# A Mamba-like macaron block on one core: x times B for four states at once, the clip and all products on GpSimd, one projection, new places in the order

## The chip, the cores and the metric

The kernel runs on one core of one Trainium2 chip. The core has four compute engines that work side by side and each take their instructions in a fixed order: TensorE (PE in the profile; its weight loads are listed as PEld), VectorE (DVE), ScalarE (ACT) and GpSimd (POOL). SyncE (SP) issues the transfers. An instruction waits on semaphores for its operands and buffers, and what stands behind it in its engine's queue waits with it. The metric is the device time of one execution in microseconds (us). Before the change it is 3603.74 us, the median of three executions (3602.82 to 3605.33).

## The reference

The input x is 32 sequences ("batches") of 512 positions and 256 channels, fp32. A block has three parts, each with a residual:

```python
x = x + 0.5 * ffn(layernorm(x))
x = x + ssm(layernorm(x))
x = x + 0.5 * ffn(layernorm(x))
```

The FFN has 704 hidden channels, and its inputs and weights go through a 4-bit quantization in blocks of 16 (scale = largest absolute value / 6, value = nearest of eight grid points, times scale):

```python
h = silu(q(x) @ q(w_gate).T) * (q(x) @ q(w_up).T)
out = q(h) @ q(w_down).T
```

The state-space part has N = 16 states per channel. A is -1 to -16, A and dt are fp32:

```python
Bm, Cm = split(x @ W_in + b_in)                  # 16 columns each
dt = softplus((x @ W_dt1 + b_dt1) @ W_dt2 + b_dt2)   # through 64 columns
dt = clip(dt, 1e-7, 1e6)
A_bar = exp(A * dt)                              # per channel and state
B_barX = expm1(A * dt) / (A * dt) * dt * Bm * x
h[t] = A_bar[t] * h[t-1] + B_barX[t]             # along the 512 positions
out = sum over states (h * Cm) + D * x
```

## The kernel before

**Tiling.** One batch is handled as four row tiles of 128 positions (`NJ`), or, in the state-space part, as two column halves of 128 channels (`NC`) by 512 positions. Everything is fp32 except the quantizer's curve, which is bf16. The weights of the FFN are loaded, quantized and transposed once, at the start (three blocks of gate and up rows, two blocks of down rows).

**The FFN** (`ffn`): a layernorm, `quantize` of the 128x1024 activations, two transposes, and then for each row tile: gate projections in two halves of 352 columns (line 676) with silu on ScalarE, up projections, the product of both, `quantize` of the 128x704 result, transposes (710), the down projection (722) and a copy out (729). The product is made by GpSimd (699) after two ScalarE copies of up out of PSUM (696); for tile 0 of the first FFN alone (`BY_DVE`) VectorE makes it straight from PSUM (692) without these copies.

**`quantize`**: VectorE takes the largest value of each block (544), the scale (546), its reciprocal (548) and the quotient (550, into PSUM); ScalarE squares and bends it (554, 556); TensorE adds and subtracts a large constant, which rounds to the grid (563); ScalarE copies out (569); GpSimd multiplies by the scale (570). The quotient lives in one PSUM buffer, "q", of which there is one, so two quantizations follow each other.

**The state-space part** (`ssm`): a layernorm, transposes, one projection for B and C (741 with `w_in_sb`, bias 745) and one to the 64 columns of dt (741 with `w_dt1_sb`, bias 752), from there dt (757), softplus on ScalarE within PSUM (761) and the clip on VectorE out of PSUM into SBUF (764). B and C are written to DRAM and come back, spread over all 128 partitions, two states at a time (780, 782). For each pair of states of a column half: exp and tanh by ScalarE (789, 792), x times B by GpSimd (796), and for each state three VectorE instructions: e (803), e times x B (806) and the scan along the positions (809). GpSimd multiplies the pair by C (812), and TensorE adds it, turned, to the sum over the states in PSUM (818). expm1 is had from exp and tanh: exp(2z) - 1 = (exp(2z) + 1) tanh(z).

x times B is one GpSimd instruction for two states and 512 positions (1024 columns), written with the state as the innermost index, so that one x element is used twice in a row:

```python
op("POOL", "x b", lambda c=c, bx=bx, bn=bn: g.tensor_tensor(
    bx().rearrange("p n l -> p l n"),
    xT()[:, c, :].unsqueeze(2).to_broadcast([P, L, NG]),
    bn().rearrange("p n l -> p l n"), ALU.mult),
```

**The order.** Nothing is issued at once. `op` records each instruction with its reads and writes, and `Plan.run` puts all of them, of all batches, in one list: of those whose inputs have been issued and whose buffers are free it always takes the one with the smallest place. The place is the entry of its name in the table `WHEN` plus `PERIOD` times its batch. So every batch has the same places, shifted, and work of several batches is interleaved: in the steady stage the FFN 0 of one batch, the state-space part of the one before it and FFN 1 of an older one run together. A place is no time; only the order follows from it, and the numbers of buffers (three PSUM buffers "pt" for all projections, transposes and small things, one "q", two or three of the others) bound how far an engine runs ahead. The list is fixed before the kernel runs. The first batch has a fill stage ahead of it, where the weights are quantized, and the last a drain.

The functions that the change touches follow, with the line numbers that the profile uses.

Of the kernel before, what the change touches and what calls it, by code (L numbers as in the profile page):

```python
# [9 lines left out]
F32 = mybir.dt.float32  # L10
# [6 lines left out]
P = 128  # L17
# [14 lines left out]
        "weights load": (7249, 7248, 7249, 7249, 6726, 6726, 6642, 6642, 6642, 6841, 6841, 6841,  # L32
        6841),
        "weights x top": (7249, 7065, 7353),
        "weights x scale": (7250, 7248, 7385),
        "weights x rinv": (7250, 7248, 7391),
        "weights x quotient": (7250, 7248, 7391),
        "weights x square": (7250, 7249, 7392),
        "weights x curve": (7250, 7249, 7392),
        "weights x grid": (7250, 7249, 7557),  # L40
        "weights x rounded": (7250, 7249, 7557),
        "weights x value": (7250, 7249, 7558),
        "weights turn": (7251, 7251, 7249, 7249, 7558, 7558),
        "weights turned": (7251, 7251, 7250, 7251, 7558, 7558),
        "weights load down": (7065, 6579),
        "weights h top": (7558, 6642),
        "weights h scale": (7571, 6642),
        "weights h rinv": (7571, 6642),
        "weights h quotient": (7571, 6643),
        "weights h square": (7590, 6643),  # L50
        "weights h curve": (7590, 6643),
        "weights h grid": (7590, 6643),
        "weights h rounded": (7590, 6643),
        "weights h value": (7795, 7065),
        "weights turn down": (7795, 7795, 7699, 7661),
        "weights turned down": (7897, 7814, 8179, 7699),
        "weights zero rows": (8077, 8345),
        "in load": (0,),
        "ffn 0 stats": (1267, 1773, 601, 2361),
        "ffn 0 mean": (1913, 2355, 1536, 3584),  # L60
        "ffn 0 var + eps": (4038,),
        "ffn 0 rstd": (4045,),
        "ffn 0 - mean": (3609,),
        "ffn 0 shift": (4249,),
        "ffn 0 normal": (4499, 5056, 6579, 4467),
        "ffn 0 x top": (6643,),
        "ffn 0 x scale": (6726,),
        "ffn 0 x rinv": (6822,),
        "ffn 0 x quotient": (6835,),
        "ffn 0 x square": (6841,),  # L70
        "ffn 0 x curve": (6873,),
        "ffn 0 x grid": (6880,),
        "ffn 0 x rounded": (6950,),
        "ffn 0 x value": (6969,),
        "ffn 0 xqT turn": (7065, 7129),
        "ffn 0 xqT turned": (7136, 7168),
        "ffn 0 tile 0 gate": (7353, 7251),
        "ffn 0 tile 0 silu": (7437, 7321),
        "ffn 0 tile 0 up": (7577, 7558),
        "ffn 0 tile 0 up silu": (7584, 7571),  # L80
        "ffn 0 tile 0 h top": (7590,),
        "ffn 0 tile 0 h scale": (7609,),
        "ffn 0 tile 0 h rinv": (7661,),
        "ffn 0 tile 0 h quotient": (7705,),
        "ffn 0 tile 0 h square": (7737,),
        "ffn 0 tile 0 h curve": (7808,),
        "ffn 0 tile 0 h grid": (7814,),
        "ffn 0 tile 0 h rounded": (7897,),
        "ffn 0 tile 0 h value": (8045,),
        "ffn 0 tile 0 turn h": (8301, 8192),  # L90
        "ffn 0 tile 0 turned h": (8352, 8339),
        "ffn 0 tile 0 down": (8397,),
        "ffn 0 tile 0 sum": (8461,),
        "ffn 0 tile 1 gate": (7385, 7392),
# [187 lines left out]
        "ffn 1 tile 3 sum": (18157,),  # L282
        "out store": (19712,),
}


class Buf:

# [598 lines left out]
```

## Time and profile before

| What | Value |
|---|---|
| Median of three executions | 3603.74 us |
| The profiled execution | 3604.13 us, span 3602.2 us |
| Granted TensorE clock over the span | 0.984 of full |
| First softplus table load / last | 123.7 us / 3408.7 us |
| Out stores, first and last issue | 395.7 us / 3598.4 us |
| Busy: PE / DVE / ACT / POOL | 3348.0 / 3409.9 / 3385.7 / 3332.3 us |
| Instructions: PE / DVE / ACT / POOL | 16604 / 5280 / 5813 / 1963 |

The page adds up the busy time of each engine over the whole span, fill and drain included; the windows view gives the same for a chosen stretch. A row of the costliest groups reads: line, engine, operation, tiles written and read, shapes and count, then the total busy time in us and the mean duration of one in ns, and last the engine's idle time just before these instructions with what ended it. A row of the waits reads: engine, tile and line that waited, what ended the wait, us in total, times, longest. Instructions of one engine overlap a little at their ends, so a group's busy time can be under its count times the mean.

### The profile page before, as it was taken

The numbers are of one execution on the slowest core, as the hardware profiler recorded it, in microseconds if no ns is written. First come the engines' busy times: TensorE is split into PE (matmuls) and PEld (weight loads), VectorE is DVE, ScalarE is ACT, GpSimd is POOL, SyncE is SP. The second block draws the span as 40 slices with busy tenths as digits, with TensorE's granted clock in tenths as the row PEclk, the third lists the DMA queues.
The fourth block names the chain that finished last, engine by engine and source line by source line (L and its number), as shares of the span: only waits on it lengthen the run. The fifth ranks groups of instructions, "written<-read, shape, count | busy, mean of one in ns | idle before, by whom it ended". The sixth has DMA issues, their size and how long they took to land. (4 is left out here: it accounts for less than half of the span.)

```text
span 3602.2 us, 51333 instructions
## 1 busy us (share of the span) xinstructions
PE 3348.0 (93%) x16604; PEld 2443.6 (68%) x16826; DVE 3409.9 (95%) x5280; ACT 3385.7 (94%) x5813; POOL 3332.3 (93%) x1963
## 2 busy tenths in 40 slices
PE   5779999999999999999999999999999999999966
PEld 3457777667767767777766776776777776777654
DVE  3699999999999999999999999999999999999992
ACT  4689999999999999999999999999999999999973
POOL 2589999999999999999999999999999999999992
PEclk9899999999999999999999999999999999999988
DMA  1354545444545545454544454444555454445440
GB/s 45 112 173 166 173 164 176 165 169 165 176 171 170 165 158 175 170 173 164 177 165 169 165 176 170 170 165 159 176 171 173 163 177 165 168 161 169 171 170 12
DMA packets 186652, 578.36 MB, mean 161 GB/s; under 512 B 19664, under 2 KB 54032, under 8 KB 186384
## 3 DMA queue, kind: packets, MB, share of 16 engines
q1 hardware_dynamic: 184816, 574.89, 46.7%
q8 instruction: 133, 2.18, 0.2%
q14 instruction: 135, 1.11, 0.1%
q10 hardware_dynamic: 1568, 0.18, 0.0%
HBM read 556.12 MB, written 18.87 MB: 160 GB/s over the span
## 5 line engine op out<-in xcount | busy, mean ns | idle before, releaser
L676 PE MATMUL pt<-w_guT,xqT 128*128 128x352 f32 x4096 | 1317.4, 466 | 26.1 <-DVE dt L764 16.3
L812 POOL TENSOR_TENSOR hs<-hs,bc 128x1024 f32<-128x1024 f32 x512 | 1214.0, 2371 | 9.3 <-DVE hs L809 2.6
L809 DVE TENSOR_TENSOR_SCAN hs<-ab,eb 128x512 f32<-128x512 f32 x1024 | 1202.4, 1197 | 4.5
L796 POOL TENSOR_TENSOR bx<-xT,bc 128x1024 f32<-128x1024 f32 x512 | 1171.2, 2294 | 30.3 <-DVE eb L806 15.9
L676 PEld LDWEIGHTS pt<-w_guT,xqT 128*128 128x128 f32 x4096 | 753.3, 192 | 409.7 <-DVE dt L764 24.0
L792 ACT ACTIVATE eb<-dt,a_half 128x512 f32<-128x512 f32 x1024 | 708.1, 700 | 36.1 <-DVE hs L809 29.5
L806 DVE SCALAR_TENSOR_TENSOR eb<-eb,a_inv,bx 128x512 f32<-128x512 f32 x1024 | 734.9, 743 | 2.7
L722 PE MATMUL pt<-w_dT,hqT 128*128 128x256 f32 x3072 | 717.0, 383 | 14.8 <-ACT hqT L715 14.8
L789 ACT ACTIVATE ab<-dt,a_sb 128x512 f32<-128x512 f32 x1024 | 700.8, 727 | 1.5
L803 DVE SCALAR_TENSOR_TENSOR eb<-ab,eb 128x512 f32<-128x512 f32 x1024 | 684.5, 682 | 11.4 <-ACT eb L792 7.6
L722 PEld LDWEIGHTS pt<-w_dT,hqT 128*128 128x128 f32 x3072 | 580.1, 192 | 140.4 <-ACT hqT L715 32.9
L818 PE MATMUL py<-ident,hs 128*128 128x128 f32 x4096 | 536.1, 276 | 26.1 <-POOL hs L812 25.8
L818 PEld LDWEIGHTS py<-ident,hs 128*128 128x128 f32 x4096 | 469.4, 142 | 102.0 <-POOL hs L812 38.3
L570 POOL TENSOR_TENSOR h_q<-h_q,h_sc 128x704 f32<-128x704 f32 x258 | 360.3, 1397 | 53.2 <-ACT h_q L569 52.6
L699 POOL TENSOR_TENSOR h<-h,sl 128x704 f32<-128x704 f32 x224 | 379.0, 1692 | 27.4 <-ACT h L696 22.4
L544 DVE TENSOR_REDUCE q<-h 128x44 f32<-128x704 f32 x258 | 227.0, 880 | 68.6 <-POOL h L699 43.8
L710 PE MATMUL pt<-ident,h_q 128*128 128x128 f32 x1536 | 237.0, 278 | 41.2 <-ACT h L696 24.1
L563 PE MATMUL q<-h_m,eye 128*128 128x192 bf16 (+1 forms) x873 | 191.6, 305 | 70.9 <-ACT h_m L556 62.0
L710 PEld LDWEIGHTS pt<-ident,h_q 128*128 128x128 f32 x1536 | 180.5, 141 | 110.3 <-ACT h L696 51.8
L563 PEld LDWEIGHTS <-eye 128*128 128x128 bf16 x1300 | 125.2, 99 | 183.9 <-issue 106.8
L715 ACT COPY hqT<-pt 128x256 f32<-128x256 f32 (+1 forms) x512 | 233.9, 487 | 6.1 <-PE pt L710 5.7
L686 ACT ACTIVATE sl<-pt 128x352 f32<-128x352 f32 x512 | 222.5, 463 | 16.6 <-PE pt L676 13.8
(78 smaller groups left out, 4134.6 us busy)
## 6 DMA issues: line engine op xcount, KB each, us to landing
bc<-rows SPq DMA_DIRECT2D x1024, 512.0 KB, 4.1
x<-in_L_attn_x_dram SPq DMA_DIRECT2D x32, 512.0 KB, 5.2
out_dram<-x SPq DMA_DIRECT2D x32, 512.0 KB, 7.3
rows<-bc SPq DMA_DIRECT2D x32, 64.0 KB, 3.4
xn<-in_L_ffn_w_up_dram SPq DMA_DIRECT2D x6, 128.0 KB, 2.2
h<-in_L_ffn_w_down_dram SPq DMA_DIRECT2D x2, 352.0 KB, 3.4
xn<-in_L_ffn_w_gate_dram SPq DMA_DIRECT2D x5, 128.0 KB, 2.2
w_dt_sb<-in_L_attn_W_dt_dram ACTq DMA_DIRECT2D x2, 64.0 KB, 5.5
```

The costliest lines, as they stand in the source:

```text
L676: pe.matmul(to()[:, :HALF], lhsT=xqT()[:, c, j * P : (j + 1) * P], rhs=w_guT()[:, c, o : o + HALF], start=(c == 0), stop=(c == NC - 1),)
L699: op("POOL", "product", lambda sl=sl, h=h: g.tensor_tensor(h(), h(), sl(), ALU.mult), [h, sl], [h])
L710: pe.transpose(pt()[:, i * P : (i + 1) * P], hq()[:, kcol[k] : kcol[k] + P], ident)
L722: pe.matmul(po()[:, :DM], lhsT=hqT()[:, k, :], rhs=w_dT()[:, k, :], start=(k == 0), stop=False,)
L789: op("ACT", "exp", lambda c=c, i=i, k=k, ab=ab: s.activation(ab()[:, i, :], dt()[:, c, :], AF.Exp, scale=a_sb[:, c, k : k + 1]), [(dt, c)] ...
L792: op("ACT", "tanh", lambda c=c, i=i, k=k, eb=eb: s.activation(eb[i](), dt()[:, c, :], AF.Tanh, scale=a_half[:, c, k : k + 1]), [(dt, c)], ...
L796: op("POOL", "x b", lambda c=c, bx=bx, bn=bn: g.tensor_tensor(bx().rearrange("p n l -> p l n"), xT()[:, c, :].unsqueeze(2).to_broadcast([P ...
L803: op("DVE", "e", lambda i=i, ab=ab, eb=eb: v.scalar_tensor_tensor(eb[i](), ab()[:, i, :], 1.0, eb[i](), ALU.add, ALU.mult), [(ab, i), eb[i ...
L806: op("DVE", "e x b", lambda c=c, i=i, k=n + i, eb=eb, bx=bx: v.scalar_tensor_tensor(eb[i](), eb[i](), a_inv[:, c, k : k + 1], bx()[:, i, : ...
L809: op("DVE", "scan", lambda i=i, h=h, ab=ab, eb=eb: v.tensor_tensor_scan(h()[:, i, :], ab()[:, i, :], eb[i](), 0.0, ALU.mult, ALU.add), [(a ...
L812: op("POOL", "h c", lambda h=h, cn=cn: g.tensor_tensor(flat(h()), flat(h()), flat(cn()), ALU.mult), [h, cn], [h])
L818: pe.matmul(py()[:, j, :], lhsT=h()[:, i, j * P : (j + 1) * P], rhs=ident, is_transpose=True, start=False, stop=False, skip_group_check=True,)
```

## The change

- **x times B** (`XG = 4`): B is loaded for four states at a time, one transfer in the place of two. GpSimd multiplies in two instructions per group of four states, each over all four states and half of the positions, with the four states innermost. Both have 1024 columns, so the number of instructions and columns per batch stays as it was (16 and 16384). C still comes two states at a time. There are two buffers of B and two of the result, each for four states.
- **The clip of dt**: softplus writes SBUF instead of PSUM, and GpSimd clips there, in place, with one instruction per column half, in place of VectorE.
- **The products**: `PRODUCT_BY_DVE` is empty. GpSimd makes the product of tile 0 of the first FFN too, and ScalarE makes the two copies of up ahead of it. (`VALUE_BY_DVE` is empty as well, so the scale product stays on GpSimd.)
- **One projection**: the weights of dt and of B and C stand side by side in one tile of 96 columns; one pair of matmuls, one PSUM buffer and one bias instruction make both.
- **The places**: all entries of `WHEN` are new, and the plan has tables of their own for the first two and the last two batches (`FIRST`, `SECOND`, `LAST_BUT_ONE`, `LAST`). `PERIOD` stays 3379.

The numbers in the tables are left out below.

```diff
-WHEN = { ... }
+WHEN = { ... }
+FIRST = { **WHEN, ... }
+SECOND = { **WHEN, ... }
+LAST_BUT_ONE = { **WHEN, ... }
+LAST = { **WHEN, ... }
+
+PRODUCT_BY_DVE = set()
+VALUE_BY_DVE = set()
+CLIP_BY = "POOL"
...
-    def __init__(self):
-        self.ops, self.slots = [], {}
+    def __init__(self, tables):
+        self.ops, self.slots, self.tables = [], {}, tables
...
-        o.at = (WHEN[o.name][k] + self.batch * PERIOD, len(self.ops))
+        table = self.tables.get(self.batch, WHEN)
+        o.at = (table[o.name][k] + self.batch * PERIOD, len(self.ops))
...
     NG = 2
+    XG = 4
     PT = 3
...
-    w_in_sb = const.tile([P, NC, 2 * N], F32, name="w_in_sb")
-    w_dt1_sb = const.tile([P, NC, R], F32, name="w_dt1_sb")
+    w_p_sb = const.tile([P, NC, R + 2 * N], F32, name="w_p_sb")
     w_dt2_sb = const.tile([R, DM], F32, name="w_dt2_sb")
-    b_in_sb = const.tile([2 * N, 1], F32, name="b_in_sb")
-    b_dt1_sb = const.tile([R, 1], F32, name="b_dt1_sb")
+    b_p_sb = const.tile([R + 2 * N, 1], F32, name="b_p_sb")
...
-    BY_DVE = {(0, 0)}
...
-    plan = Plan()
+    plan = Plan({0: FIRST, 1: SECOND, NB - 2: LAST_BUT_ONE, NB - 1: LAST})
...
-                if (which, j) in BY_DVE:
+                if (which, j) in PRODUCT_BY_DVE:
...
-        def project(to, w):
+        def project():
             for c in range(NC):
-                pe.matmul(to, lhsT=w[:, c, :], rhs=xT()[:, c, :], start=(c == 0), stop=(c == NC - 1))
-
-        op("PE", "bc", lambda: project(pbc()[: 2 * N, :], w_in_sb), [xT], [pbc])
-        bc = new(sp, [2 * N, L], F32, "bc", 1)
-        op("ACT", "bc bias", lambda: s.activation(
-            bc(), pbc()[: 2 * N, :], AF.Identity, bias=b_in_sb), [pbc], [bc])
+                pe.matmul(pbc()[: R + 2 * N, :], lhsT=w_p_sb[:, c, :], rhs=xT()[:, c, :],
+                          start=(c == 0), stop=(c == NC - 1))
+
+        op("PE", "project", project, [xT], [pbc])
+        bc = new(sp, [R + 2 * N, L], F32, "bc", 1)
+        op("ACT", "project bias", lambda: s.activation(
+            bc(), pbc()[: R + 2 * N, :], AF.Identity, bias=b_p_sb), [pbc], [bc])
         rows = new(dr, [2 * N, L], F32, "rows", 2)
-        op("SP", "rows", lambda: nc.sync.dma_start(rows(), bc()), [bc], [rows])
-        p1 = new(ps, [P, L], F32, "pt", PT)
-        op("PE", "dt1", lambda: project(p1()[:R, :], w_dt1_sb), [xT], [p1])
-        r1 = new(sp, [R, L], F32, "r1", 1)
-        op("ACT", "dt1 bias", lambda: s.activation(
-            r1(), p1()[:R, :], AF.Identity, bias=b_dt1_sb), [p1], [r1])
+        op("SP", "rows", lambda: nc.sync.dma_start(rows(), bc()[R:, :]), [bc], [rows])
         dt = new(sp, [P, NC, L], F32, "dt", 2)
         p2 = [new(ps, [P, L], F32, "pt", PT) for _ in range(NC)]
         for c in range(NC):
             op("PE", "dt2", lambda c=c: pe.matmul(
-                p2[c](), lhsT=w_dt2_sb[:, c * P : (c + 1) * P], rhs=r1(), start=True, stop=True),
-               [r1], [p2[c]])
+                p2[c](), lhsT=w_dt2_sb[:, c * P : (c + 1) * P], rhs=bc()[:R, :],
+                start=True, stop=True), [bc], [p2[c]])
         for c in range(NC):
-            op("ACT", "softplus", lambda c=c: s.activation(
-                p2[c](), p2[c](), AF.Softplus, bias=b_dt2_sb[:, c : c + 1]),
-               p2[c:], [p2[c]])
-            op("DVE", "dt", lambda c=c: v.tensor_scalar(
-                dt()[:, c, :], p2[c](), 1e-7, 1e6, ALU.max, ALU.min), [p2[c]], [(dt, c)])
+            if CLIP_BY == "POOL":
+                op("ACT", "softplus", lambda c=c: s.activation(
+                    dt()[:, c, :], p2[c](), AF.Softplus, bias=b_dt2_sb[:, c : c + 1]),
+                   p2[c:], [(dt, c)])
+                op("POOL", "dt", lambda c=c: g.tensor_scalar(
+                    dt()[:, c, :], dt()[:, c, :], 1e6, 1e-7, ALU.min, ALU.max),
+                   [(dt, c)], [(dt, c)])
...
             for n in range(0, N, NG):
-                bn, cn = (new(st, [P, NG, L], F32, f"bc{i}", 2) for i in range(2))
-                op("SP", "load b", lambda n=n, bn=bn: nc.sync.dma_start(
-                    bn(), rows()[n : n + NG, :].partition_broadcast(P)), [rows], [bn])
+                if n % XG == 0:
+                    bn, bx = (new(st, [P, XG, L], F32, tag, 2) for tag in ("bn", "bx"))
+                    op("SP", "load b", lambda n=n, bn=bn: nc.sync.dma_start(
+                        bn(), rows()[n : n + XG, :].partition_broadcast(P)), [rows], [bn])
+                    for o in range(0, L, L * NG // XG):
+                        t = slice(o, o + L * NG // XG)
+                        op("POOL", "x b", lambda c=c, bx=bx, bn=bn, t=t: g.tensor_tensor(
+                            bx()[:, :, t].rearrange("p n l -> p l n"),
+                            xT()[:, c, t].unsqueeze(2).to_broadcast([P, L * NG // XG, XG]),
+                            bn()[:, :, t].rearrange("p n l -> p l n"), ALU.mult),
+                           [(xT, c), bn], [(bx, o)])
+                cn = new(st, [P, NG, L], F32, "cn", 2)
                 op("SP", "load c", lambda n=n, cn=cn: nc.sync.dma_start(
                     cn(), rows()[N + n : N + n + NG, :].partition_broadcast(P)), [rows], [cn])
...
-                bx = new(st, [P, NG, L], F32, "bx", 2)
-                op("POOL", "x b", lambda c=c, bx=bx, bn=bn: g.tensor_tensor(
-                    bx().rearrange("p n l -> p l n"),
-                    xT()[:, c, :].unsqueeze(2).to_broadcast([P, L, NG]),
-                    bn().rearrange("p n l -> p l n"), ALU.mult),
-                   [(xT, c), bn], [bx])
...
                     op("DVE", "e x b", lambda c=c, i=i, k=n + i, eb=eb, bx=bx: v.scalar_tensor_tensor(
-                        eb[i](), eb[i](), a_inv[:, c, k : k + 1], bx()[:, i, :],
+                        eb[i](), eb[i](), a_inv[:, c, k : k + 1], bx()[:, k % XG, :],
                         ALU.mult, ALU.mult), [eb[i], bx], [eb[i]])
```

## The prediction

> **What bounds the kernel now.** I read the page's first two parts, then a window over ten batches, then the waits in that window, then the costliest groups with shapes kept apart, and last the two ends.
>
> The page, part 1 and the first rows of part 2 (busy us, share, instructions; tenths in 40 slices of 90 us):
> ```profile
> PE 3348.0 (93%) x16604; PEld 2443.6 (68%) x16826; DVE 3409.9 (95%) x5280; ACT 3385.7 (94%) x5813; POOL 3332.3 (93%) x1963
> ...
> DVE  3699999999999999999999999999999999999992
> ACT  4689999999999999999999999999999999999973
> POOL 2589999999999999999999999999999999999992
> ```
> Four engines look alike because the ends are averaged in. Softplus loads its table once per batch. The row of line 761 for a middle window (1000 to 2200 us), and the windows view over the ten batches that it marks:
> ```profile
> L761 ACT ACT_TABLE_LOAD  x11: 1283/1283/1283, 1070.7 to 2134.9; - x11
> ```
> ```profile
> 1070.70:2134.80 1064.10, 1027.29 (x5172) 753.63 (x5240) 1058.12 (x1641) 1049.80 (x1811) 1038.24 (x611) 1.00 0.50 169
> ```
> Eleven loads from 1070.7 to 2134.9 us are ten batches of 106.41 us. After the window's length stand PE, PEld, DVE, ACT, POOL, then the clock. Per batch: DVE 105.8, ACT 105.0 to 105.1, POOL 103.8, PE 102.7. The waits in the same window: VectorE has none, and ScalarE's are
> ```profile
> ACT x L729 <- PE pt L726: 2.9, 10, 0.3
> ACT xn_s L522 <- POOL shift L519: 2.2, 10, 0.2
> ACT eb L792 <- DVE hs L809: 2.0, 10, 0.2
> ```
> So VectorE sets the pace: 105.8 us of work and 0.6 us between instructions make 106.41 us. ScalarE follows 0.9 us behind: 105.1 us of work and 0.4 us of gaps under 60 ns make 105.5 us, and the rest of its time is waiting that VectorE's pace causes. GpSimd has 2.6 us to spare, TensorE 3.6.
>
> **The change, part by part**, in us per batch of the steady stage. The groups that price it:
> ```profile
> L812 POOL TENSOR_TENSOR hs<-hs,bc 128x1024 f32<-128x1024 f32 x512 | 1214.0, 2371 | 9.3 <-DVE hs L809 2.6 <-DMA bc<-rows 1.5 <-PE pt L676 1.2
> L796 POOL TENSOR_TENSOR bx<-xT,bc 128x1024 f32<-128x1024 f32 x512 | 1171.2, 2294 | 30.3 <-DVE eb L806 15.9 <-DMA bc<-rows 14.2
> L699 POOL TENSOR_TENSOR h<-h,sl 128x704 f32<-128x704 f32 x224 | 379.0, 1692 | 27.4 <-ACT h L696 22.4 <-issue 2.7 <-DVE h_sc L546 1.6
> L696 ACT COPY h<-pt 128x352 f32<-128x352 f32 x448 | 191.2, 450 | 7.9 <-PE pt L676 7.6
> L570 POOL TENSOR_TENSOR x_q<-x_q,x_sc 128x1024 f32<-128x1024 f32 x67 | 129.7, 1936 | 60.5 <-ACT x_q L569 60.5
> L741 PE MATMUL pt<-xT,w_in_sb 128*32 128x512 f32 x128 | 60.9, 598 | 0.0
> L764 DVE TENSOR_SCALAR dt<-pt 128x512 f32<-128x512 f32 x64 | 40.4, 671 | 14.9 <-ACT pt L761 14.9
> L692 DVE TENSOR_TENSOR h<-pt,sl 128x352 f32<-128x352 f32 x64 | 32.8, 512 | 13.3 <-PE pt L676 10.2
> L752 ACT ACTIVATE r<-pt,b_dt_sb 64x512 f32<-64x512 f32 x32 | 22.2, 693 | 2.2 <-PE pt L741 2.2
> L745 ACT ACTIVATE bc<-pt,b_in_sb 32x512 f32<-32x512 f32 x32 | 21.2, 664 | 1.2 <-PE pt L741 1.2
> ```
> *VectorE* loses the clip (40.4/32 = 1.26) and the two products of tile 0 of the first FFN (32.8/32 = 1.02): 106.41 - 2.28 = 104.1. It stops being the bound.
>
> *ScalarE* gains two up copies in their place (2 x 191.2/448 = +0.85) and loses one of the two bias instructions (21.2/32 = -0.66; the merged one has 96 rows, and the rows of 32 and 64 take nearly the same, 664 and 693 ns). Softplus, writing SBUF instead of PSUM, I leave at its 662 ns. The list of the changed kernel has nine table loads per steady batch, as before, and three more in the whole run (one in the fill, two in the drain, 1.28 us each, beside idle ScalarE time there). So its floor is 105.5 + 0.2 = 105.7: the next bound is only 0.7 us below the old one.
>
> *TensorE* loses one projection, 60.9/32 = 1.9: 102.8 + 0.4 - 1.9, about 101.3. It sets nothing. Softplus into SBUF also frees a PSUM slot one step earlier; TensorE waited 5.2 us for the clip's in ten batches, time that it has to spare.
>
> *GpSimd* gains the product of tile 0 (+1.69) and two clips, and its x times B changes shape. The number of x-times-B instructions (16) and their elements (1024) stay; the innermost run is 4 states, with x repeated 4 times, instead of 2. No row shows either price.
> - Clip, 128x512, one input: from below, the only one-input operation here (the identity's affine select, 292 ns for 128 columns, less the 203 ns of a 4-column tensor_tensor, is 0.70 ns a column): 0.56 us. From above, at the two-stream rate of the 1024-column h times c ((2371 - 203)/1024 = 2.12 ns): 1.29 us. I take 0.75, nearest to the one-input row (0.87 with the 98 ns memset as its fixed part).
> - x times B: from above 2371 ns, two full streams without any repeat; from below 1936 ns, the scale product, whose second operand is repeated 16 times. Repeats of 2 give 2294. With the fixed 203 ns off, that is 2.04 ns a column at 2 and 1.69 at 16; halfway in doublings, one of three steps, gives 1.92 at 4: 2.17 us. I take it; 16 x (2.17 - 2.294) = -2.0.
>
> Sum: 103.8 + 1.7 + 1.5 - 2.0 = 105.0; with the ends of both prices 100.9 to 109.3. At the taken values GpSimd lies 0.7 us under ScalarE, with no spare time for much waiting.
>
> The Trainium skill, "GPSIMD Engine Reference", section "Performance pitfalls for Q7 kernels", says that reads with a step over 8 bytes cost about 2.9 instead of 1.9 cycles an element. x times B steps by 2048 bytes in both kernels, and its 2294 ns lie under the 2371 ns of the contiguous h times c, so this trace doesn't show the penalty. By the rule (1.2 GHz on the same page) an estimate is 2.7 us each, 113 us of GpSimd work per batch, and a kernel of about 3790 us.
>
> *Clip on GpSimd as a wait.* It now stands in GpSimd's queue (behind an x value, an x-times-B and h-times-c pair and a product of older work), and ScalarE's exp waits for it. In the list, ScalarE has one silu with its table load, two tanh, a square and three more silu between softplus and the first exp, some 6 us; the clip needs 0.75 us plus at most the h value before the second (1.4). I cost it at nothing; without that cover it is up to 1.4 us a batch, on the engine that is then the bound.
>
> *Loads of B*: half as many, 1 MB each, two buffers as before; a group of four states lasts 106.4/8 = 13 us and a 512 KB load lands in 4.1 us, so two times that is covered. B's loads were waiting for buffers, not the reverse (GpSimd waited 2.3 us for them in ten batches). SP gets shorter. Nothing.
>
> *Orders, steady.* The new lists run the same stages at the same lags as the old ones, with neighbours exchanged. The old order let VectorE wait for nothing while the others had 0.9, 2.6 and 3.6 us to spare; in the new one ScalarE is the bound and the others have 1.6 (VectorE), 0.7 and 4.4. I allow 0.2 us of waiting: 105.9 us. Between softplus of batch 1 and of batch 30 lie 29 periods: 29 x (105.9 - 106.41) = -15. Bounds: floor 105.7, -21; GpSimd at its upper prices, 109.3, +84.
>
> *The drain.* In the waits of the last 90 us:
> ```profile
> DVE q L544 <- POOL h L699: 32.0, 2, 20.8
> DVE q L544 <- ACT h_q L569: 10.8, 2, 7.5
> ```
> The last FFN runs tile by tile, and the absolute maximum waits for the product on GpSimd. The old list put one gate of tile 1 before tile 0's up (4 matmuls, about 1.9 us) and h value 0 and six gate or up projections before product 1 (tile 0's quantizing ended at 3559.8, tile 1's began at 3567.3). The new list removes both. But TensorE is busy 44.4 of the 56 us from 3542, so most of the gain would run into it: -5, between -9 and, since other steps moved too, +5.
>
> *The fill.* Quantizing is one chain through a single PSUM buffer; at the third block of gate/up weights it stood 41.5 to 46.2 us because its small tile waited for a PSUM slot, and at tiles 2 and 3 it waited 3 to 4 us each for products. The new list copies the turned weights earlier and puts products before h values. TensorE is busy 50.6 of 64 us there: -4, between -10 and +5.
>
> Sum: 3604.1 (profiled execution: span 3602.2 and 1.9 around it) - 15 - 4 - 5 = 3580; this execution is 0.4 above the median of 3603.74, so **3580**.
>
> **The rivals.**
> - *Both ends and the floor in full* (0.20): 105.7 us a batch (-21), fill -8, drain -8: 3567. For it: before, the bound ran without any wait. Against: TensorE's own share at the ends.
> - *ScalarE keeps its waits* (0.12): the 1.0 us that it waits now is in the order and not in VectorE's pace; 105.7 + 1.0 = 106.7, 29 x 0.3 = +9, ends -9: 3604, no change. For it: each of the three waits occurs once in every batch. Against: they are short, 0.2 to 0.3 us, as of an engine with time to spare.
> - *GpSimd becomes the bound* (0.16), the slower side: x times B stays at 2294 ns. Then 103.8 + 1.7 + 1.5 = 107.0, 29 x 0.6 = +17, less 5 for the ends: 3616; at 2371 ns 108.3 us a batch, 3653. It decides from about 106.7 us of GpSimd work, that is 2.27 us per x times B. For it: most of the saving must come from a shape that no row shows. Against: 2 repeats are already cheaper than none, and 16 much cheaper.
>
> **How the numbers follow.** Forecast 0.52 (3572 to 3596), full gain 0.20 (3558 to 3572), no change 0.12, GpSimd bound 0.16. A measurement tells about 0.2% (7 us) from no change. Faster 0.72, within 0.2% 0.12, slower 0.16. The range 3558 to 3618 leaves out about one in ten above (GpSimd at its higher prices) and less below.
>
> **What would show it.** Right: softplus loads 105.7 to 106.1 us apart; ScalarE over 99% busy in the middle window, VectorE near 97.5%; the x-times-B row at 2.1 to 2.2 us and the clip at 0.6 to 0.9; VectorE's wait for products in the drain shorter. Wrong: x times B at 2.29 us or more, or GpSimd over 99% busy, or exp waiting for the clip by over 0.3 us a batch.

## The result

The changed kernel takes 3767.08 us (median of 3763.97 to 3768.47), the one before 3604.05 us in the same runs: the ratio is 1.0451, 95% interval 1.0433 to 1.0469. The prediction was 3580 us, faster. It is 163 us slower.

The profile of the changed kernel, the page's part 1 and the rows of part 2 that were shown of the kernel before:

```profile
PE 3336.0 (89%) x16501; PEld 2445.0 (65%) x16698; DVE 3387.0 (90%) x5152; ACT 3423.8 (91%) x5848; POOL 3562.6 (95%) x2059
...
DVE  4799999999999999999999999999999999999984
ACT  5789999999999999999999999999999999999974
POOL 3799999999999999999999999999999999999994
```

GpSimd (POOL) rose from 3332 to 3563 us of work, and VectorE and ScalarE, 95 and 94% busy before, are at 90 and 91%. The softplus table load marks the batches again (now on line 1670); first a window from 1000 to 2300 us, then the windows view over the ten batches it gives (length, PE, PEld, DVE, ACT, POOL):

```profile
L1670 ACT ACT_TABLE_LOAD  x11: 1283/1283/1283, 1111.2 to 2237.3; - x11
```

```profile
1111.20:2237.30 1126.10, 1023.66 (x5140) 753.72 (x5200) 1050.17 (x1601) 1061.35 (x1821) 1110.03 (x641) 0.99 0.48 160
```

A batch takes 112.61 us instead of 106.41. GpSimd works 111.0 of them. In the same ten batches VectorE, which waited for nothing before, waits for ScalarE's tanh, for x times B and for the product (what waited, for what: us in total, times, longest):

```profile
DVE eb L1722 <- ACT eb L1717: 42.3, 76, 1.4
DVE eb L1725 <- POOL bx L1701: 14.4, 10, 1.5
DVE q L1451 <- POOL h L1611: 11.2, 12, 1.4
```

The groups that answer to those of the prediction:

```profile
L1701 POOL TENSOR_TENSOR bx<-xT,bn 128x1024 f32<-128x1024 f32 x512 | 1318.5, 2582 | 10.5 <-DMA bn<-rows 8.3
L1731 POOL TENSOR_TENSOR hs<-hs,cn 128x1024 f32<-128x1024 f32 x512 | 1208.5, 2366 | 8.6 <-PE pt L1588 2.3
L1611 POOL TENSOR_TENSOR h<-h,sl 128x704 f32<-128x704 f32 x256 | 432.1, 1688 | 51.2 <-ACT h L1608 43.1
```

```profile
L1673 POOL TENSOR_SCALAR dt<-dt x64: 612/612/615, 106.8 to 3633.2; 128x512 f32<-128x512 f32 x64
```

x times B takes 2582 ns with four states innermost, where it took 2294 with two; all 512 of them lie between 2553 and 2671 ns, those of the fill and the drain included. GpSimd's other rows (h times c, the product) kept the durations that they had in the kernel before. The sum by the prediction's own steps, with the two measured prices: 103.8 + 1.7 (product) + 1.2 (two clips of 612 ns) + 16 x 0.288 = 4.6 make 111.3 us of GpSimd work; 111.0 were measured.

Where the 163.6 us of the span (3765.8 - 3602.2) lie, by the first and the last softplus load (104.7 and 3582.7 us, before 123.7 and 3408.7): the fill became 19.0 us shorter, the 31 intervals between the loads 193.0 us longer, and the drain 10.4 us shorter (183.1 after 193.5). In the last 90 us VectorE's two longest waits, for the product and for ScalarE's copy out of q, shrank from 32.0 and 10.8 us to

```profile
DVE q L1451 <- POOL h L1611: 21.7, 2, 18.0
DVE q L1451 <- ACT h_q L1481: 9.7, 2, 6.4
```

### The profile page after: what moved, and what is told of

Its sections match the earlier page's. It is cut to its first block, busy times and chain, and to the rows that moved or that the text cites. A ratio compares the mean times of both kernels' runs of the same rounds, so it can differ in the third digit from the quotient of the medians.

```text
span 3765.8 us, 50230 instructions
## 1 busy us (share of the span) xinstructions
PE 3336.0 (89%) x16501; PEld 2445.0 (65%) x16698; DVE 3387.0 (90%) x5152; ACT 3423.8 (91%) x5848; POOL 3562.6 (95%) x2059
## 4 chain that ended last, share of the span: by engine, by line
POOL 38%; PE 23%; DVE 17%; ACT 12%; issue 9%; DMA 0%; POOLq 0%; SPq 0%; DVEq 0%; ACTq 0%
POOL hs L1731 14%; PE pt L1588 12%; POOL bx L1701 11%; DVE hs L1728 5%; POOL h_q L1482 5%; DVE eb L1725 4%; POOL h L1611 3%; PE py L1737 3%; POOL x_q L1482 3%; PE pt L1634 3%; DVE eb L1722 2%; ACT ab L1714 2%; DVE q L1457 2%; ACT eb L1717 2%; PE pt L1622 2%
## 5 line engine op out<-in xcount | busy, mean ns | idle before, releaser
L1588 PE MATMUL pt<-w_guT,xqT 128*128 128x352 f32 x4096 | 1339.4, 471 | 12.6 <-ACT sl L1598 6.5
L1701 POOL TENSOR_TENSOR bx<-xT,bn 128x1024 f32<-128x1024 f32 x512 | 1318.5, 2582 | 10.5 <-DMA bn<-rows 8.3
L1731 POOL TENSOR_TENSOR hs<-hs,cn 128x1024 f32<-128x1024 f32 x512 | 1208.5, 2366 | 8.6 <-PE pt L1588 2.3
L1725 DVE SCALAR_TENSOR_TENSOR eb<-eb,a_inv,bx 128x512 f32<-128x512 f32 x1024 | 745.1, 747 | 49.9 <-POOL bx L1701 42.0
L1714 ACT ACTIVATE ab<-dt,a_sb 128x512 f32<-128x512 f32 x1024 | 720.8, 727 | 2.0 <-DVE hs L1728 0.5
L1634 PEld LDWEIGHTS pt<-w_dT,hqT 128*128 128x128 f32 x3072 | 571.4, 191 | 125.0 <-ACT hqT L1627 37.0
L1737 PE MATMUL py<-ident,hs 128*128 128x128 f32 x4096 | 544.7, 282 | 74.7 <-POOL hs L1731 74.6
L1737 PEld LDWEIGHTS py<-ident,hs 128*128 128x128 f32 x4096 | 485.8, 146 | 163.0 <-POOL hs L1731 95.0
L1611 POOL TENSOR_TENSOR h<-h,sl 128x704 f32<-128x704 f32 x256 | 432.1, 1688 | 51.2 <-ACT h L1608 43.1
L1622 PEld LDWEIGHTS pt<-ident,h_q 128*128 128x128 f32 x1536 | 170.7, 142 | 238.9 <-POOL h_q L1482 117.9
```

The costliest lines, as they stand in the source:

```text
L1588: pe.matmul(to()[:, :HALF], lhsT=xqT()[:, c, j * P : (j + 1) * P], rhs=w_guT()[:, c, o : o + HALF], start=(c == 0), stop=(c == NC - 1),)
L1611: op("POOL", "product", lambda sl=sl, h=h: g.tensor_tensor(h(), h(), sl(), ALU.mult), [h, sl], [h])
L1634: pe.matmul(po()[:, :DM], lhsT=hqT()[:, k, :], rhs=w_dT()[:, k, :], start=(k == 0), stop=False,)
L1701: op("POOL", "x b", lambda c=c, bx=bx, bn=bn, t=t: g.tensor_tensor(bx()[:, :, t].rearrange("p n l -> p l n"), xT()[:, c, t].unsqueeze(2).t ...
L1714: op("ACT", "exp", lambda c=c, i=i, k=k, ab=ab: s.activation(ab()[:, i, :], dt()[:, c, :], AF.Exp, scale=a_sb[:, c, k : k + 1]), [(dt, c)] ...
L1725: op("DVE", "e x b", lambda c=c, i=i, k=n + i, eb=eb, bx=bx: v.scalar_tensor_tensor(eb[i](), eb[i](), a_inv[:, c, k : k + 1], bx()[:, k % ...
```

## The experiments

Two theories stood against each other. "Price": the shape of x times B costs what its row says, GpSimd becomes the bound by it, and the rest of the prediction held. "Order": the new places, made for some other balance, or the clip and the product in GpSimd's queue, cost waits by themselves.

### What a shape of x times B costs

The changed kernel, with each of the eight groups of four states of a batch in another shape, each on a line of its own; two of the eight:

```diff
-bx()[:, :, t].rearrange("p n l -> p l n"),                                # read and written at a step of 2048 bytes
-bn()[:, :, t].rearrange("p n l -> p l n"), ALU.mult),
+# shape 4: written side by side, B read at the step
+flat(bx())[:, o * 1024 : o * 1024 + 1024].rearrange("p (l n) -> p l n", n=4), ...
+# shape 5: B read side by side, written at the step
+flat(bn())[:, o * 1024 : o * 1024 + 1024].rearrange("p (l n) -> p l n", n=4), ALU.mult)
```

> The changed kernel with x times B in eight shapes, one for each of the eight groups of four states of a batch, each of 1024 columns and on its own line; in the shapes that read or write the tile as if states lay side by side the products are not the reference's. It is a price list. Shapes: (0) four states innermost, as changed: 2.58 us again. (1) two states innermost: 2.29, as before the change. (2) positions innermost, four states by 256, and (3) two by 512: both 2.37, as h times c, if only the count of streams matters; nearer 2.0 if a repeat of x in the outer index is also saved. (4) B read at a 2048-byte step, result written side by side; (5) B read side by side, result written at a step; (6) both side by side; (7) eight states innermost at a 1024-byte step. Theory 'reading at a step': 5 and 6 are cheap (1.9 to 2.2), 4 stays at 2.58 and 7 is above it. Theory 'writing at a step': 4 and 6 cheap, 5 at 2.58. Theory 'short inner runs': all of 0, 4, 5, 6 dear and 7 cheaper than 0.

The groups of its GpSimd instructions on these lines (line 1704 is shape 0, 1706 shape 1, 1710 shape 3, 1712 shape 4, 1714 shape 5, 1716 shape 6, 1719 shape 7):

```profile
L1712 POOL TENSOR_TENSOR bx<-xT,bn 128x1024 f32<-128x1024 f32 x64 | 164.8, 2576 | 0.1
L1704 POOL TENSOR_TENSOR bx<-xT,bn 128x1024 f32<-128x1024 f32 x64 | 163.4, 2578 | 2.1 <-DMA bn<-rows 1.9
L1719 POOL TENSOR_TENSOR bx<-xT,bn 128x1024 f32<-128x1024 f32 x64 | 161.8, 2531 | 0.0
L1710 POOL TENSOR_TENSOR bx<-xT,bn 128x1024 f32<-128x1024 f32 x64 | 151.7, 2371 | 3.7 <-DMA bn<-rows 3.3 <-DVE stats L1414 0.4
L1706 POOL TENSOR_TENSOR bx<-xT,bn 128x1024 f32<-128x1024 f32 x64 | 145.0, 2290 | 5.5 <-DMA bn<-rows 5.3
L1714 POOL TENSOR_TENSOR bx<-xT,bn 128x1024 f32<-128x1024 f32 x64 | 131.5, 2056 | 0.6 <-POOL h L1611 0.5
L1716 POOL TENSOR_TENSOR bx<-xT,bn 128x1024 f32<-128x1024 f32 x64 | 129.7, 2028 | 3.3 <-DMA bn<-rows 2.0 <-DVE q L1451 1.0 <-POOL h L1611 0.2
```

The read decides. Written side by side but read at the step, it stays at 2576 ns; read side by side but written at the step, it falls to 2056, and with both side by side (shape 6) to 2028. Positions innermost (shapes 2 and 3) take 2360 and 2371 ns, as h times c: a repeat of x in the outer index saves next to nothing. Eight states innermost at a step of 1024 bytes (2531 ns) are hardly better than four. Theory "reading at a step" was right in each of its numbers but one, shape 7, which was to lie above shape 0 and lies a little under it.

A second list separates the step from the repeat. Its shapes are all written side by side; five of the eight:

```diff
+k == 0: xx (x repeated 2), flat(bn())[:, span].rearrange("p (l n) -> p l n", n=2)          # side by side
+k == 1: xx, bn()[:, 2 * o : 2 * o + 2, :].rearrange("p n l -> p l n")                      # step 2048 bytes
+k == 2: x4 (x repeated 4), flat(bn()).rearrange("p (l n s) -> p s l n", s=2, n=4)[:, o]      # step 8 bytes
+k == 3: x4, flat(bn()).rearrange("p (l n s) -> p s l n", s=4, n=4)[:, 2 * o : 2 * o + 2]     # step 16 bytes
+k == 6: no repeat: bn side by side, times bn at a step of 2048 bytes
```

> Second price list, as the first (products are not the reference's; all 1024 columns, all written side by side but for nothing else). (0) two innermost, B side by side: about 2.05 to 2.15. (1) two innermost, B read at 2048 bytes: 2.29 if the write plays no part here either. (2) four innermost, B read at a step of 8 bytes; (3) at 16 bytes: 2.03 and 2.58 if the penalty begins between them, both 2.58 if any step costs. (4) x and B both repeated four times: under 1.9. (5) two side-by-side streams without a repeat: 2.37. (6) one such stream and one read at 2048 bytes, no repeat: 2.9 if penalties and repeats add up, 2.58 if the repeat of x is hidden behind the stepped read. (7) x repeated 16 times, B side by side: 1.94, as the scale product.

The same view (line 1709 is shape 0, 1711 shape 1, 1713 shape 2, 1715 shape 3, 1722 shape 5, 1724 shape 6, 1727 shape 7; shape 5 is two side-by-side streams without a repeat, shape 7 repeats x 16 times):

```profile
L1724 POOL TENSOR_TENSOR bx<-bn 128x1024 f32<-128x1024 f32 x64 | 185.2, 2896 | 3.0 <-DMA bn<-rows 2.0 <-DVE q L1451 0.9
L1715 POOL TENSOR_TENSOR bx<-xT,bn 128x1024 f32<-128x1024 f32 x64 | 163.7, 2559 | 1.2 <-DMA bn<-rows 0.9
L1722 POOL TENSOR_TENSOR bx<-bn 128x1024 f32<-128x1024 f32 x64 | 152.3, 2380 | 2.0 <-POOL h L1611 1.9
L1711 POOL TENSOR_TENSOR bx<-xT,bn 128x1024 f32<-128x1024 f32 x64 | 145.1, 2291 | 1.6 <-DMA bn<-rows 1.4
L1709 POOL TENSOR_TENSOR bx<-xT,bn 128x1024 f32<-128x1024 f32 x64 | 136.1, 2150 | 2.1 <-DMA bn<-rows 2.0
L1713 POOL TENSOR_TENSOR bx<-xT,bn 128x1024 f32<-128x1024 f32 x64 | 131.9, 2062 | 0.0
L1727 POOL TENSOR_TENSOR bx<-xT,bn 128x1024 f32<-128x1024 f32 x64 | 123.7, 1935 | 2.3 <-DMA bn<-rows 2.3
```

Two effects show, and with four states innermost or no repeat at all they add up. A repeat of x saves: 2380 ns with none, 2150 with two, 2062 with four (at 8 bytes), 1935 with sixteen. A stepped read costs about 500 ns: 2062 to 2559 between steps of 8 and 16 bytes, 2380 to 2896 without a repeat. Four states innermost got the larger saving (88 ns over two) and the whole penalty. Two states innermost at the same 2048 bytes pay only 141 ns of it (2291 after 2150); why so little, no run here settles.

So the rule of the Trainium skill that the prediction set aside ("GPSIMD Engine Reference", "Performance pitfalls for Q7 kernels") has its cliff where these rows have it, between 8 and 16 bytes. Its size is about 0.5 ns a column here, where an estimate from that page, one cycle at its 1.2 GHz, is 0.83 ns.

### The one shape undone

```diff
-for o in range(0, L, L * NG // XG):
-    t = slice(o, o + L * NG // XG)      # four states, half of the positions
+for o in range(0, XG, NG):
+    t = slice(o, o + NG)                # two states, all positions
...                                      # and bn()[:, t, :], bx()[:, t, :], all of x, in the instruction
```

> The changed kernel with one thing undone: x times B with two states innermost and all 512 positions, two instructions for a group of four (loads, buffers, places, clip, products and projection stay as changed). Theory 'price': the loss is the shape of x times B alone, 16 x 0.29 = 4.6 us a batch on GpSimd; then GpSimd has 111.0 - 4.6 = 106.4 us of work, a batch takes 106.5 to 107.2 us, and with the shorter fill and drain (19 and 10 us) the kernel is at 3575 to 3600 us, under the 3604 of before. Theory 'order': the new places, made for another balance, or the clip and the product in GpSimd's queue cost waits of their own; then it stays above 3640 us.

Measured: 3614.25 us, ratio 1.0024 (1.0013 to 1.0036). Ten middle batches of the paired kernel, load marks and windows view:

```profile
L1670 ACT ACT_TABLE_LOAD  x11: 1283/1283/1283, 1070.3 to 2147.0; - x11
```

```profile
1070.30:2147.00 1076.70, 1012.91 (x5200) 747.73 (x5200) 1046.96 (x1601) 1055.34 (x1821) 1064.16 (x641) 1.00 0.50 167
```

GpSimd works 106.4 us of a batch, as expected, but the batch takes 107.67, 0.5 more than the top of the expectation, and the kernel stays above the one before. Of the loss of 163 us the shape is 153. The remaining 10 are made of a fill that is 18.4 us shorter, a drain 14.2 us shorter and 43.6 us more in between: with GpSimd at 106.4 us there is no gain to be had over 106.41, and 1.2 us of waits and gaps come on top.

### The cheap read with everything else as changed

Only the read of B is exchanged for one side by side, so the elements of B come in the wrong order.

```diff
-bn()[:, :, t].rearrange("p n l -> p l n"), ALU.mult),
+flat(bn())[:, t.start * XG : t.stop * XG].rearrange("p (l n) -> p l n", n=XG), ALU.mult),
```

> The changed kernel whole, all its places too, but x times B reads B's tile as if the four states lay side by side (so B's elements come in another order and the output is not the reference's; count, columns and result places stay). By the price list one costs 2.06 instead of 2.58 us, close to the 2.17 of the prediction. Theory 'price': GpSimd falls from 111.0 to about 102.7 us a batch, ScalarE binds at 105.9 to 106.5, and with the fill and drain of the changed kernel it is at 3560 to 3580 us, so the rest of the prediction held. Theory 'order': the new places cost waits by themselves; above 3600.

Measured: 3566.52 us, ratio 0.9899 (0.9885 to 0.9912). The windows view over ten middle batches:

```profile
1059.80:2121.80 1062.00, 1012.71 (x5200) 745.67 (x5200) 1045.47 (x1601) 1050.74 (x1820) 1026.76 (x641) 1.00 0.50 169
```

This is the kernel that the prediction had in mind, with a price that is still a little lower than the 2.17 us that it took:

```profile
L1701 POOL TENSOR_TENSOR bx<-xT,bn 128x1024 f32<-128x1024 f32 x512 | 1041.6, 2043 | 12.4 <-DMA bn<-rows 7.8 <-POOL h L1611 2.0 <-DVE hs L1729 1.0
```

GpSimd is down to 102.7 us, ScalarE is the busiest at 105.1, and a batch takes 106.20 us, where 105.9 was forecast. Same places, same clip, same product, same projection: theory "order" is out as the cause of the loss, and "price" accounts for 200 us between this kernel and the changed one.

### One part alone in the kernel before

Two parts were put into the kernel before, with its old places.

```diff
-op("DVE", "dt", lambda c=c: v.tensor_scalar(dt()[:, c, :], p2[c](), 1e-7, 1e6, ALU.max, ALU.min), ...
+op("POOL", "dt", lambda c=c: g.tensor_scalar(dt()[:, c, :], dt()[:, c, :], 1e6, 1e-7, ALU.min, ALU.max), ...
```

> The kernel before with one part of the change: softplus writes SBUF and GpSimd clips there at the old place. VectorE 105.8 - 1.3 = 104.5 us of work a batch, GpSimd 103.8 + 1.2 = 105.0, ScalarE as before. Theory 'busy time decides': the bound falls to ScalarE's 105.5, up to 25 us faster, 3578 to 3604. Theory 'the order decides once two engines are close': a new wait in the old order eats it; slower than 3604 by up to 50 us.

Measured: 3640.54 us, ratio 1.0094 (1.0077 to 1.0111). VectorE has less to do (104.9 us a batch, before 105.8), and a batch is longer, 107.61 us. VectorE's waits in 1100 to 2200 us begin with

```profile
DVE h L692 <- PE pt L676: 19.3, 19, 1.3
```

The product of tile 0, which VectorE reaches earlier now that the clip is gone, waits for its up projection, 1.9 us a batch, and everything behind it in the queue with it. Theory "busy time decides" failed; a wait took the place of the work.

The other part, x times B by fours with clip, products, projections and places of before:

```diff
-bn, cn = (new(st, [P, NG, L], F32, f"bc{i}", 2) for i in range(2))
+if n % XG == 0:
+    bn, bx = (new(st, [P, XG, L], F32, tag, 2) for tag in ("bn", "bx"))
+    ... two instructions of four states by 256 positions, as changed
```

> The kernel before with one part of the change: B loaded and multiplied four states at a time, states innermost; all else as before (clip and products by VectorE, two projections, old places). Theory 'price': GpSimd gets 103.8 + 4.6 = 108.4 us a batch, 2 us over the old period, so at least +58 us: 3662 us, up to 3700 with waits, since the old order was not made for it. Theory 'order': the shape costs little by itself, 3604 to 3625 us.

Measured: 4398.05 us, ratio 1.2207, far over the expectation. x times B took 2577 ns here too, so the price is the same, but by the expectation's sum it explains only some 60 us. The second half of a group kept the place of a later pair. With the place of the first:

```diff
+WHEN["ssm x b"] = tuple(t for t in WHEN["ssm x b"][::2] for _ in range(2))
```

> As before_fours, but both halves of a group of four have the place of the first: in before_fours the second half kept the place of a later pair, and the first pair's e times B waited for it. Theory 'second half too late': it falls to 3660 to 3720 us, where GpSimd's 108.4 us a batch put it. Rival: something else in the old order; still above 4000.

Measured: 3928.11 us, ratio 1.0902. More than half of the excess was that place, but not all, and a batch still takes some 117 us, in which GpSimd works 108.3. Both expectations failed by their size. As a measure of the price these two are of no use; they show that a part moved without its places measures the places.

### The clip and the load of GpSimd

With the paired shape, GpSimd was relieved in two ways.

```diff
-CLIP_BY = "POOL"
+CLIP_BY = "DVE"
```

> As the one before the last (two states innermost), and the clip goes back to VectorE, with softplus in PSUM. GpSimd loses 1.2 us a batch (105.2), VectorE gains 1.3. Theory 'price' with GpSimd as the bound of the paired kernel: a batch gets shorter by up to 0.6 us, to where ScalarE binds at about 105.9 to 106.2, 5 to 18 us less than with the clip on GpSimd. Rival 'the clip in GpSimd's queue was a wait': more than 20 us less. Second rival: the clip's place in VectorE's queue delays the scans, equal or slower.

Measured: 3753.91 us, ratio 1.0417: 140 us more than with the clip on GpSimd. I then supposed that the PSUM slots were held too long, since softplus writes PSUM in this variant:

```diff
-op("POOL", "dt", lambda c=c: g.tensor_scalar(dt()[:, c, :], dt()[:, c, :], ...
+op("DVE", "dt", lambda c=c: v.tensor_scalar(dt()[:, c, :], dt()[:, c, :], ...
```

> Two states innermost, clip by VectorE as in pairs_clip, but softplus writes SBUF and VectorE clips there, so the two PSUM slots are free after softplus. Theory 'PSUM slot': the 140 us that pairs_clip lost to pairs came from the slots held until VectorE reached its clip; then this is at 3575 to 3605 us, with GpSimd at 105.2 us of work a batch. Rival 'place in VectorE's queue': it stays above 3700 us.

Measured: 3756.22 us, ratio 1.0424. The slots were not it. VectorE's waits of this run, from 1100 to 2200 us, begin with

```profile
DVE dt L1673 <- ACT dt L1670: 24.5, 10, 2.5
```

VectorE comes to the clip 2.5 us before softplus is done, in each batch, and stands. A batch takes 112.6 us instead of 107.7; how the other half of the 5 us arises was not followed. On GpSimd the clip is 1.2 us of work a batch, and no wait of ScalarE in the ten batches of the changed kernel names it: as a wait I had costed it there at nothing, and that held.

The second way takes the scale product of tile 0 of the first FFN, one of eight tiles, off GpSimd:

```diff
-VALUE_BY_DVE = set()
+VALUE_BY_DVE = {(0, 0)}
```

> Two states innermost, and the scale product of tile 0 of the first FFN is made by VectorE straight from PSUM, without ScalarE's copy out (the changed kernel's own switch VALUE_BY_DVE, for one tile of eight). GpSimd loses 1.4 us a batch (105.0), ScalarE 0.75 (about 105.2), VectorE gains 0.9 (105.0 with its gaps). Theory 'GpSimd binds the paired kernel': a batch takes 105.8 to 106.6 instead of 107.4, 25 to 45 us less than pairs: 3568 to 3590, under both kernels. Rival: the single buffer q, held until VectorE gets to it, costs more than that; 3614 or more.

Measured: 3626.56 us, ratio 1.0065, 12 us more than pairs. GpSimd works 105.2 us of a batch, 1.3 less than in pairs, and a batch takes 108.1 us. So in the paired kernel GpSimd's work alone did not set the 107.7 us; the order around it did its part. The rival's time came true, but not its reason as far as the waits show: the longest new ones of ScalarE and GpSimd are for VectorE's scan and layernorm (18.8 us each in 1100 to 2200 us), not for q.

### The tables for the ends

```diff
-plan = Plan({0: FIRST, 1: SECOND, NB - 2: LAST_BUT_ONE, NB - 1: LAST})
+plan = Plan({0: FIRST, 1: SECOND})
```

> The paired kernel with the last two batches on the steady table instead of tables of their own; the first two keep theirs. In pairs the drain after the last softplus table load is 179 us, before it is 193.5. Theory 'the own tables make the short drain': back to 190 to 200 us, so 10 to 20 us over pairs, 3624 to 3634. Rival: the product placed ahead of the older scale product in all tables is what shortened it; the same as pairs within 5 us.

Measured: 3637.29 us, ratio 1.0084, 23 us over pairs. The drain after the last softplus load is 198.7 us (span 3633.9 less 3435.2) where pairs has 179.3. So the own tables for the last two batches make the short drain, and the rival, the place of the product in all tables, is out.

### The cheap read with B in its own order

The price list pointed to a faster kernel: B brought side by side. Three ways were tried.

```diff
+# interleaved: B projected a second time with positions on the rows, biased by VectorE
+pe.matmul(pb()[:, j * N : (j + 1) * N], lhsT=xT()[:, c, j * P : (j + 1) * P], rhs=w_p_sb[:, c, R : R + N], ...)
+rowsb = new(dr, [N // XG, L, XG], F32, "rowsb", 2)       # four states side by side
```

> The changed kernel with B brought into the layout that the price list asks for, with the right values: B is projected a second time with positions on the rows (eight small matmuls a batch), biased by VectorE, stored in DRAM with the four states of a group side by side, and loaded that way; x times B then reads it side by side and writes as changed. Theory 'price': 2.05 us for one x times B and about the time of side_by_side, 3566 us, plus what the new steps cost on engines with time to spare and their delay at the first batch: 3565 to 3590, under the kernel before. Rival: stores of 16 bytes or the extra PSUM slot hold up the state-space part; 3600 or more.

Measured: 3665.30 us, ratio 1.0160. x times B is cheap (GpSimd 102.6 us a batch), but a batch takes 108.85 us. TensorE went from 101.3 to 103.9 us, and ScalarE's first wait is now for the transposes of the next FFN, which stand behind the new matmuls (20.0 us in 1100 to 2200 us).

```diff
+# interleaved_dma: stored by the transfers alone, in 4-byte elements
+nc.sync.dma_start(rowsb()[k].rearrange("l n -> n l"), bc()[R + k * XG : R + (k + 1) * XG, :])
```

> The changed kernel with B stored in DRAM with the four states of a group side by side, by the transfers alone: four of 8 KB a batch with 4-byte elements in place of B's half of the one of 64 KB; no new work on TensorE, VectorE or PSUM, and the values are right. 2048 elements each at the 8 to 9 ns that the trace shows for packets of 4 and 16 bytes, over 16 engines, are about 1 us. Theory 'price': x times B at 2.05 us, a batch at 106.0 to 106.7 us as in side_by_side, 3563 to 3580, faster than both kernels. Rival 'the second projection of interleaved was not what cost it 100 us, the way of B through DRAM was': 3620 or more.

Measured: 5215.02 us, ratio 1.4468. The row of that store on SyncE's queue, and GpSimd's longest wait:

```profile
L1668 SPq DMA_DIRECT2D rowsb<-bc x128: 617/12630/19389, 103.3 to 5011.3; - x128
```

```profile
POOL hs L1746 <- DMA cn<-rows: 1523.6, 33, 52.6
```

To issue one store of 2048 elements holds the queue for 12.6 us (median; from 0.6 to 19.4), four for some 50 us a batch, and the loads of C stand behind them. A batch takes 157.1 us on average (the softplus loads run from 104.8 to 4974.7 us), some 50 more than with the cheap read alone. I had priced the elements (9 ns each over 16 engines) and not the issue.

```diff
+# interleaved_turn: the rows that the one projection gave, turned by four small transposes behind dt
+pe.transpose(pb()[:, j * N : (j + 1) * N], bc()[R : R + N, j * P : (j + 1) * P], ident[R : R + N, R : R + N])
```

> The changed kernel with the cheap read of B and right values by a third way: B's 16 rows, as they come from the one projection, are turned by four small transposes behind the projection of dt, copied out by VectorE and stored in 16-byte pieces. TensorE gains about 1 us a batch in place of the 2.6 of interleaved's second projection, and nothing stands ahead of the transposes of the next FFN. Theory 'the added projection in TensorE's queue cost interleaved its 100 us': 3570 to 3600 us, under the kernel before. Rival 'any added step there, with its PSUM slot, costs as much': 3630 or more.

Measured: 3694.60 us, ratio 1.0251. From 1200 to 2300 us VectorE waits 20.6 us for x times B, and x times B 31.3 us for B's load: B now comes by a longer way, and later than the places assume. A batch takes 108.5 us there. Both this run and the first of the three land where their rivals put them (an added step with its PSUM slot, small stores), but no run takes the slot, the stores and the later B apart. With B in its own order none of the three beats the kernel before; places made for one of them were not tried.

## Why the prediction was wrong

**The step that failed is the price of x times B.** "I take it; 16 x (2.17 - 2.294) = -2.0" should have been +4.6 us a batch, and the bound "from above 2371 ns, two full streams without any repeat" was no bound: the row of 2294 ns that I interpolated from already held part of a penalty for reading at a step, and the row that I interpolated towards (1936 ns) reads side by side. What I took for the effect of two repeats, 2371 to 2294, was a saving of 230 ns and a penalty of 141. The Trainium skill's rule, weighed in the same place and set aside with that row, gave 3790 us; 3767 was measured. That it came so near is partly luck, since its penalty of one cycle, by the estimate 0.83 ns a column, is too large: these rows show 0.5. The argument against it, that the stepped read of the kernel before isn't slower than a contiguous one, compared two rows that differ in two things.

**The rival on the slower side** named the mechanism, GpSimd as the bound, and its threshold, 2.27 us for one x times B. Its prices ended at 2371 ns and 3653 us. With the measured 2582 ns its sum gives 111.3 us a batch, 29 x 4.9 = 142 us and 3741; the batch took 112.6, 1.3 us more. Of the prediction's signs of being wrong, x times B at 2.29 us or more came true; GpSimd is busy for 98.6% of a batch, just under the 99% named there, and no exp waits for the clip.

**VectorE** stopped being the bound, as said. 104.1 us a batch were forecast, gaps included; without them it works 104.5 in the kernel with the cheap read and 105.0 in the changed one.

**ScalarE**: a floor of 105.7 us was forecast, and in the kernel with the cheap read, where it binds, a batch takes 106.20. Softplus into SBUF takes 694 ns, not the 662 that I left it at.

**The clip**: 612 ns, taken 750, within its bounds; as a wait it cost nothing on GpSimd. On VectorE, in the paired kernel with the new places, it costs 140 us more.

**The loads of B and the one projection** cost nothing that the runs show: GpSimd waited 1.8 us for B in ten batches, TensorE works 101.3 us a batch in pairs and in the kernel with the cheap read.

**The orders, steady**: 0.2 us of waiting over ScalarE's floor of 105.7 was allowed; with the cheap read it is 0.5 (106.2), and with pairs 1.2 us over GpSimd's work.

**The ends** were forecast at -4 and -5 us and came to -19 and -10, with the cheap read -18 and -18. The direction was right, but all four lie outside the ranges given (no lower than -10 and -9), so the kernel with the cheap read comes out 13 us under the 3580 although its batch is 0.3 us longer than forecast. In the fill, the wait of a quantization behind the turned weights went from 10.3 to 2.0 us, as the prediction read from the list. The group of the 128x1024 absolute maximum, first of the kernel before, then of the changed one:

```profile
L544 DVE TENSOR_REDUCE pt<-xn 128x64 f32<-128x1024 f32 x67 | 81.0, 1209 | 25.1 <-ACT xn L522 10.9 <-ACT w_guT L624 10.3 <-DMA xn<-in_L_ffn_w_gate_dram 4.0
```

```profile
L1451 DVE TENSOR_REDUCE pt<-xn 128x64 f32<-128x1024 f32 x67 | 81.3, 1213 | 6.8 <-ACT xn L1429 4.9 <-ACT w_guT L1536 2.0
```

## What to carry to other kernels

A price between two rows is interpolated only when the rows differ in the one thing that is interpolated; where a rule names a second thing in which they differ, that thing gets a price of its own, and the range reaches it. When four engines stand within a few per cent of each other, 0.3 us on an instruction that runs 16 times a batch chooses the bound. And in an order that is fixed ahead, work taken off an engine can come back as a wait, in its own queue or in the one that the work moves to: three changes here made a kernel slower by relieving its busiest engine (the clip taken off VectorE before; the clip, and a scale product, taken off GpSimd in pairs).

## What the runs showed of the hardware

- GpSimd, 1024 fp32 columns of tensor_tensor: 2380 ns for two side-by-side streams, 2150, 2062 and 1935 with one of them repeated 2, 4 (read at 8 bytes) and 16 times in a row. Repeating both, four times each, gives 2023, hardly less than 2028 for one (shape 6 of the first list).
- In such an instruction, with four elements innermost or no repeat, reading one operand at a step of 16 or of 2048 bytes costs about 0.5 ns a column (2559 after 2062 ns, 2896 after 2380), 8 bytes hardly anything (2062 after 2028); a write at a step of 2048 bytes costs 0.03 (2056 after 2028). Reading with two elements innermost at 2048 bytes costs 0.14 (2291 after 2150).
- GpSimd's tensor_scalar with two operations takes 612 ns for 512 columns.
- A store of 2048 elements of 4 bytes holds SyncE's queue 12.6 us at its issue (median in interleaved_dma); one of 512 elements of 16 bytes 0.5 us (median in interleaved).
